# Expert feed-forward: weight rooms refilled by halves, eight groups summed in one accumulator bank, and the last choice rearranged

## Chip, cores and metric

The kernel runs on one core of a Trainium2 chip, in one launch. The metric is the device time of one execution in microseconds (us), as a median of runs. A profile of one further execution gives durations and waits; its own time stands beside it below. Engine names are those of the profile: PE (TensorE matmul), PEld (its weight loads), ACT (ScalarE), DVE (VectorE), POOL (GpSimd), SP (the engine that issues most DMAs).

## What is computed

The input x has shape [4, 128, 64, 64]: 4 batches of 4096 tokens with 128 channels, float32. Layer 0 is a convolutional attention and the first half of layer 1 a running-softmax attention with 8 heads; both are untouched. The change concerns the feed-forward at the end, where 64 experts choose tokens:

```python
logits = jnp.einsum('bsd,ed->bse', x, gate_w) + gate_b      # x: normalised tokens
probs = jax.nn.softmax(logits, axis=1)                      # over the 4096 tokens
vals, idx = jax.lax.top_k(probs.transpose(0, 2, 1), K)      # K = 8 tokens per expert
...
pooled = jnp.einsum('bked,bke->bed', gathered, topv)
h = jnp.concatenate([pooled.transpose(1, 0, 2), ones], axis=-1)
h = jax.nn.gelu(jnp.einsum('ebd,edh->ebh', h, weight1), approximate=False)
h = jnp.concatenate([h, ones], axis=-1)
out = jnp.einsum('ebh,eho->ebo', h, weight2)
...
outputs = outputs.at[jnp.arange(Bn)[:, None], flat_idx].add(weighted)
```

Each expert is 128 → 512 → 128. Per batch it sees one pooled vector, so an expert works on 4 vectors only, but its weights are 512 KB (256 KB for each of the two layers), 33.5 MB for all 64. The result is added to the tokens, and the tokens are turned back to channel-major order for the output.

## The kernel before, in words

Tokens stay in SBUF in one tile `t`, cut into NB = 32 blocks of 512 tokens (NBLK = 8 per batch, CPB = 4 chunks of 128). The gate's logits of batch b lie in `env.lg[b]` with 128 partitions (two token halves × 64 experts) and 8 × 256 columns.

The attention loop (`loop`, L2048) runs over the blocks with six blocks of lag. `make_plan` (L1989) hangs the gate's steps on slots of that loop: `gate_norm`, `gate_turn`, `gate_logits` for each block, `merge_half`, `merge_halves` (the eight best logits), `candidate_rows` (L1317, where they stand, L1321), `gathers` (L1329, POOL fetches those eight token rows by indirect DMA), `exps`, `count`, `select` and `pool` for finished batches. For the last batch all this can only end once the last block has left the attention, so `last_choice` (L1436) does it by hand: `outputs` (L1180) has made the last block; ACT takes early exponentials of the seven older blocks (`early_sums`, L1413), the gate of the last block follows (L1234, L1241, L1261, L1274, L1280, L1288), four blocks are turned back in between (`turn_early`, L1425), the candidates are weighed and spread (L1377), eight matmuls per batch with the gathered rows make the pooled vectors (L1482), the sums go through two small matmuls (L1489, L1504), and L1509 writes `f_pooled`. `put_early` (L1431) and an exponential over the whole batch (L1513) follow. `late_choice` (L1515), called by `experts`, is `count` (L1348, a check on how many tokens pass the threshold) and `select` (L1356, which zeroes all unchosen tokens in `f_lg`).

`experts` (L1570) takes the 64 experts in EG = 16 groups of QG = 4. In one group:

- `first`: four matmuls of 512 columns into a `kv` bank (L1588; the trace shows two instructions for each float32 matmul), each expert on its own 32 output partitions, then a copy by ACT (L1593);
- `turn`: four transposes (L1599), add of the bias on DVE (L1603), gelu on ACT (L1608), each over 128×512;
- `second`: 16 matmuls (32 instructions) into bank `o` (L1615), copied by DVE (L1621);
- four reloads (`load_into`, L1556): the rooms of this group's four experts are filled with the next experts not yet loaded, one DMA of 512 KB each, issued by SP;
- four matmuls with 0/1 matrices `zz` that move the group's rows to (half, expert) order and add them up over all groups in bank `t` (L1625).

On TensorE the order is `turn(g)`, two blocks turned back (`turn_back`: four transposes into bank `x` L1567, copied by ACT L1568), `first(g+1)`, `second(g)`. There is one bank `x`, so the second `turn_back` waits for the copy of the first. Twenty experts are loaded before the groups begin (some while the attention still runs), the other 44 through `load_into`. After the groups DVE scales and adds bias (L1649) into `env.eo`.

`stores` (L1654) then makes the scatter as a matmul: for each block `f_sct` = `env.eo` times the masked `f_lg` (L1660) into one of two `kv` buffers, added to the turned-back tokens by DVE (L1666), and every second block SP issues one 512 KB DMA to the output (L1669).

Order: TensorE's instructions run in the order in which the code issues them (a manual schedule, L2122 on). ACT, DVE and POOL are in code order within `loop` and `last_choice`; in `experts` and `stores` a scheduler places their instructions, and it may place one of these ahead of the last instructions of `last_choice`. `select`, `count` and the bias product L1644 are such instructions. SP's DMAs are in code order. PSUM buffers by tag: `x`, `t`, `o`, `sm` one each, `kv` two.

## Time and profile before

| | |
|---|---|
| median of three runs | 2341.73 us (2339.94 to 2343.78) |
| profiled execution, its own time | 2340.21 us |
| its span in the trace | 2338.3 us |
| mean granted TensorE clock | 0.993 |
| busy over the span: PE, DVE, ACT, POOL | 97%, 62%, 47%, 8% |
| attention loop ends on TensorE | at about 2191.7 us |
| first `first` matmul of the expert groups (f_ph, L1588) | at 2210.53 us |
| first matmul of the stores (f_sct, L1660) | at 2307.38 us |
| last output DMA issued, landed | 2331.9, about 2334.5 us |

So the part that the change touches is about the last 145 us of the span. The page's line of the TensorE clock has, for each of 40 slices of the span, the granted share of full speed in tenths (9 stands for all of it); its line of the DMA has the mean busy share of 16 DMA engines in the same slices. A row of a table of stretches names the stretch in us and its length, then for PE, PEld, DVE, ACT and POOL the busy time and the number of instructions, then the granted clock, the DMA share and the GB/s. A group row names line, engine, operation, output and inputs, shapes and count, then total busy us and mean ns of one, then the idle time just before these and what ended it. In the chain of waits each row is a start, a length and what ran: where a row follows another, the second was waiting for the first. "issue" is time in which an engine waited for nothing that the trace shows.

### The profile page before, as it was taken

The page shows a single profiled execution, that of the slowest core. Times are in us where ns is not written, and L with a number is a line of the kernel's source. Part 1 is how long each engine was busy: PE and PEld are TensorE (multiplying, and loading weights), DVE is VectorE, ACT ScalarE, POOL GpSimd, SP SyncE. Part 2 cuts the span into 40 slices and gives each one's busy share as a digit, 9 for nine tenths or more (in the row PEclk, how much of TensorE's full clock was granted, in tenths as well). Part 3 has the DMA queues.
Part 4 walks back from the last instruction along what each step waited for, and adds up shares of the span by engine and source line. Part 5 has one row for each costly group of instructions (what it writes and reads, how often), then busy time and mean ns, then how long its engine had stood idle before and what let it go on. Part 6 is the DMA issues. An engine that isn't in the chain of part 4 may idle for free.

```text
span 2338.3 us, 43371 instructions
## 1 busy us (share of the span) xinstructions
PE 2259.9 (97%) x18530; PEld 1187.3 (51%) x18530; DVE 1452.7 (62%) x2345; ACT 1095.1 (47%) x1329; POOL 183.5 (8%) x340
## 2 busy tenths in 40 slices
PE   7999999999999999999999999999999999999877
PEld 3544444444444444444444444456656656666554
DVE  7666566555665655565565555668776777865514
ACT  3343333434333443334454444455666666656531
POOL 0000000000000000000000000012122132133300
PEclk9999999999999999999999999999999999999799
DMA  2000010000010000010000000111121121143494
GB/s 80 27 12 17 9 44 12 13 8 9 17 44 9 14 11 9 9 43 9 9 5 10 5 5 5 29 42 42 38 64 50 40 73 48 40 122 96 150 356 185
DMA packets 72587, 105.82 MB, mean 45 GB/s; under 512 B 8512, under 2 KB 44352, under 8 KB 72384
## 3 DMA queue, kind: packets, MB, share of 16 engines
q1 hardware_dynamic: 70784, 99.81, 13.5%
q8 instruction: 147, 2.41, 0.4%
q0 software_dynamic: 1024, 2.10, 0.4%
q10 hardware_dynamic: 576, 1.05, 0.1%
q14 instruction: 56, 0.46, 0.1%
HBM read 79.60 MB, written 17.04 MB: 41 GB/s over the span
## 4 chain that ended last, share of the span: by engine, by line
PE 89%; DVE 5%; ACT 3%; DMA 2%; issue 1%; POOL 0%; SPq 0%; ACTq 0%; DVEq 0%; POOLq 0%
PE av L1837 37%; PE sc L1812 18%; PE f_pv L1128 9%; PE f_pk L973 8%; PE f_pt L1151 3%; PE f_po L1174 2%; PE pd L1863 1%; PE pa L1785 1%; PE pe L1759 1%; PE f_po L1185 1%; ACT f_e1a L980 1%; PE f_eo L1625 1%; DMA x<-in_x_dram 1%; PE f_ph L1588 1%; PE f_eo L1615 1%
## 5 line engine op out<-in xcount | busy, mean ns | idle before, releaser
L1837 PE MATMUL av<-pr,am 64*128 64x512 f32 x4096 | 977.6, 592 | 2.4 <-ACT pr L1817 2.4
L1817 ACT ACTIVATE pr<-sc 128x1024 f32<-128x1024 f32 x512 | 523.6, 1023 | 781.6 <-PE sc L1812 770.5
L1824 DVE TENSOR_TENSOR acc<-acc,pr 128x1024 f32<-128x1024 f32 x480 | 586.5, 1222 | 485.1 <-ACT pr L1817 480.8
L1837 PEld LDWEIGHTS av<-pr,am 64*128 64x128 f32 x4096 | 401.9, 187 | 472.8 <-issue 458.1
L1812 PE MATMUL sc<-e,e 64*128 64x512 f32 x2048 | 535.0, 591 | 3.3 <-DMA e<-side 3.3
L1812 PEld LDWEIGHTS sc<-e,e 64*128 64x128 f32 x2048 | 201.5, 187 | 234.6 <-issue 229.2
L1128 PE MATMUL f_pv<-f_held,f_ama 128*32 128x256 f32 x4096 | 237.8, 381 | 5.3 <-ACT f_e1a L980 4.6
L973 PE MATMUL f_pk<-f_held,f_ama 128*128 128x512 f32 x512 | 234.9, 603 | 0.0
L1133 ACT ACTIVATE f_amb<-f_pv 128x1024 f32<-128x1024 f32 x128 | 130.7, 1023 | 125.0 <-PE f_pv L1128 125.0
L981 DVE TENSOR_TENSOR f_e1a<-f_e1a,f_held 128x1024 f32<-128x1024 f32 x128 | 157.3, 1230 | 48.1 <-ACT f_e1a L980 47.8
L980 ACT ACTIVATE f_e1a<-f_pk 128x1024 f32<-128x1024 f32 x128 | 129.9, 1025 | 119.4 <-PE f_pk L973 55.6
L1128 PEld LDWEIGHTS f_pv<-f_held,f_ama 128*32 128x32 f32 x4096 | 129.6, 110 | 99.4 <-ACT f_e1a L980 10.9
L982 DVE TENSOR_REDUCE f_e1a<-f_e1a 128x8 f32<-128x1024 f32 x128 | 155.2, 1217 | 3.5
L973 PEld LDWEIGHTS f_pk<-f_held,f_ama 128*128 128x128 f32 x512 | 92.5, 190 | 108.6 <-issue 101.0
L1092 POOL COPY f_held<-f_e1a 32x32 f32<-32x32 f32 x128 | 30.7, 240 | 895.1 <-DVE f_e1a L1074 559.1
L1151 PE MATMUL f_pt<-f_amb,f_held 128*32 128x128 f32 x1920 | 83.6, 278 | 0.8 <-ACT f_amb L1133 0.8
L918 POOL MEMSET f_held<- 128x1024 f32 x1 | 1.0, 956 | 1036.6 <-DVE xn L1750 1036.6
L1151 PEld LDWEIGHTS f_pt<-f_amb,f_held 128*32 128x32 f32 x1920 | 60.4, 110 | 10.4 <-issue 5.2
L1190 DVE TENSOR_TENSOR t<-t,f_po 128x512 f32<-128x512 f32 x32 | 22.0, 687 | 55.6 <-PE f_po L1185 55.6
L956 ACT ACTIVATE f_xl<-t,ln_nb,ln_rs 128x128 f32<-128x128 f32 x128 | 52.8, 490 | 0.8 <-PE pa L1785 0.8
L1261 ACT ACTIVATE f_x<-t,f_gnb,f_grs 128x128 f32<-128x128 f32 x126 | 51.3, 482 | 0.4 <-DVE f_gnb L1242 0.4
L1821 DVE COPY acc<-pr 128x1024 f32<-128x1024 f32 x32 | 22.2, 694 | 39.3 <-ACT pr L1817 39.3
(269 smaller groups left out, 1835.6 us busy)
## 6 DMA issues: line engine op xcount, KB each, us to landing
f_e2a<-f_rd SPq DMA_DIRECT2D x128, 128.0 KB, 3.1
xr<-in_xtok_dram SPq DMA_DIRECT2D x32, 256.0 KB, 2.8
out_dram<-t SPq DMA_DIRECT2D x16, 512.0 KB, 3.0
f_table<-f_x SPq DMA_DIRECT2D x62, 128.0 KB, 2.2
f_held<-in_fw_dram SPq DMA_DIRECT2D x14, 512.0 KB, 6.3
f_e1a<-in_fw_dram SPq DMA_DIRECT2D x13, 512.0 KB, 6.1
x<-in_x_dram SPq DMA_DIRECT2D x12, 512.0 KB, 5.7
f_amb<-in_fw_dram SPq DMA_DIRECT2D x12, 512.0 KB, 5.8
```

The costliest lines, as they stand in the source:

```text
L956: nc.scalar.activation(xl[:, c, :], t[:, b * NCH + i, :], AF.Identity, bias=ln_nb[:, b, i : i + 1], scale=ln_rs[:, b, i : i + 1],)
L973: nc.tensor.matmul(pk[:, i, :], xt_at(n)[:, bass.ts(c, P)], env.wks[:, bass.ts(i, BLK)], start=True, stop=True,)
L980: nc.scalar.activation(flat, pk.rearrange("p i x -> p (i x)"), AF.Silu)
L981: nc.vector.tensor_mul(ks, ks, env.qb)
L982: nc.vector.tensor_reduce(s[:, (n % GB) * CPB + c, :], ks, AX.X, ALU.add)
L1128: nc.tensor.matmul(pv[a * CH : (a + 1) * CH, i, :], xt_at(m)[:, bass.ts(c * NA + i, CH)], env.wvs[:, bass.ts(a, HH * C)], start=True, stop ...
L1133: nc.scalar.activation(env.amb[:, bass.ts(c, HD)], pv.rearrange("p i x -> p (i x)"), AF.Silu)
L1151: nc.tensor.matmul(env.pt[i * CH : (i + 1) * CH, :], lhs, rhs, start=i not in env.begun, stop=False, skip_group_check=True,)
L1812: nc.tensor.matmul(sc[:, u, :], e2[halves[u], p, :], e1[halves[u], cols], start=True, stop=True,)
L1817: nc.scalar.activation(pr, sc, AF.Exp)
L1824: nc.vector.tensor_add(acc, acc, pr)
L1837: nc.tensor.matmul(av, am[h, j, :], pr[h, u, :], start=(j == 0), stop=(j == NCH - 1))
```

## The change

In `last_choice`: `early_sums` with its separate sums and `put_early` are gone. Ten blocks instead of four are turned back here (`fill`, `put_back`): six of them before the gate of the last block, into `kv`, `t` and `o`, four more between its steps; ACT or DVE copies each back. One exponential over the whole batch (ACT, L1473 of the new file) now gives the sums, and stands ahead of the pooling; the candidates are spread in two halves, the pooling matmuls four before and four after the last block's own selection, and some copies go from ACT to DVE. `outputs` adds the last block in two halves, and `candidate_rows` of the last batch is one slot earlier in the plan.

In `experts`: the rooms are refilled by halves. The first layer's half of a room (256 KB) is refilled right after `first` of its group, the second layer's half after `second`, by separate DMAs; 21 experts instead of 20 are loaded before. The second layers of eight groups accumulate in one bank: `hold` holds two tiles in which every column but the group's own four per expert is zero, so each group adds to its own rows of `env.eh`. DVE's bias add and ACT's gelu work on those columns only (128×64 in place of 128×512), POOL clears a group's columns before a tile is used again. The moving matmuls (`spread`) run twice in all, not 16 times. `turn_back` alternates between banks `t` and `x`, and 22 blocks are left to it: two per group for six groups, then one.

In `stores`: for every fifth block (six of 32) ACT copies the product out of PSUM and POOL adds it; the first two and the last two blocks are stored singly.

In the new file TensorE's order in a group is still `turn(g)`, `turn_back`, `first(g+1)`, `second(g)`. On DVE the built program has this order at the end of the last choice: copy of the selected block (L1491), first half of `count`, reciprocal of the sums (L1503), second half of `count`, L1505, `select` (L1358), L1514, the bias product, and then the product that writes `f_pooled` (L1515). Before, the two halves of `count` and `select` stood behind that product.

The diff, cut to its core:

```diff
...
+            step = CPB if m + 1 < NB else CPB // 2
...
+            for x4 in range(0, CPB, step):
+                view = t[:, bass.ds(b * NCH + k * CPB + x4, step), :]
+                nc.vector.tensor_add(view, view, env.po[:, x4 : x4 + step])
...
-        def gate_turn(m):
+        def gate_turn(m, copy=nc.scalar.copy):
...
-            nc.scalar.copy(gxt_at(m), ptr.rearrange("p c x -> p (c x)"))
+            copy(gxt_at(m), ptr.rearrange("p c x -> p (c x)"))
...
-        def early_sums():
...
-        def turn_early(n):
...
+        def fill(n, tag, half=0):
...
+            if tag == "kv":
+                if half == 0:
+                    env.two = ps.tile([P, 2, BLK], F32, tag="kv", name=f"f_etb_{n}", bufs=2)
+                dst = env.two[:, half, :]
+            else:
+                dst = ps.tile([P, BLK], F32, tag=tag, name=f"f_etb_{n}")
             for c in range(CPB):
...
+                    dst[:, bass.ts(c, P)], t[:, b * NCH + k * CPB + c, :], ident
+                )
+            fillers[n] = (env.two, half) if tag == "kv" else (dst, None)
...
+        def put_back(n, copy, count=1):
+            src, half = fillers[n]
+            at = t[:, bass.ds(n * CPB, count * CPB), :].rearrange("p i x -> p (i x)")
+            if count == 2:
+                src = src.rearrange("p n x -> p (n x)")
+            elif half is not None:
+                src = src[:, half, :]
+            copy(at, src)
...
-            early_sums()
+            act, dve = nc.scalar.copy, nc.vector.tensor_copy
+            for n, tag in enumerate(("kv", "kv", "kv", "kv", "t", "o")):
+                fill(n, tag, n % 2)
+            put_back(0, act, 2)
             gate_root(m, 1)
             gate_close(m, 1)
             gate_norm(m, split=True)
-            turn_early(0)
-            turn_early(1)
-            gate_turn(m)
...
+            put_back(2, act, 2)
+            gate_turn(m, dve)
+            fill(6, "kv")
             gate_logits(m)
-            turn_early(3)
+            put_back(4, dve)
+            fill(7, "kv", 1)
             late = st["cand"][:, bass.ts(k, 8)]
             pw = sm("f_pw1", 8)
             nc.tensor.matmul(pw, env.swap, late, start=True, stop=True)
+            fill(8, "kv")
+            fill(9, "kv", 1)
...
-            nc.scalar.activation(chd, lg, AF.Exp, bias=neg, accum_out=s31)
             st["ce"] = ce = small_tile(b, "ce", 17, bufs=1)
             nc.scalar.activation(ce, both[:, 0:17], AF.Exp, bias=neg)
-            fac = small_tile(b, "fac", 1, bufs=1)
-            nc.scalar.activation(fac, top0[:, 0:1], AF.Exp, bias=neg)
+            nc.scalar.activation(chd, lg, AF.Exp, bias=neg)
+            put_back(5, act)
+            put_back(6, act, 2)
+            st["sums"] = sums = small_tile(b, "sums", 4, bufs=1)
+            nc.scalar.activation(
+                flat_lg(b, 0, NBLK), flat_lg(b, 0, NBLK), AF.Exp, bias=neg,
+                accum_out=sums[:, 0:1],
+            )
+            put_back(8, act, 2)
+            cw = weigh_candidates(b)
+            dd = spread_candidates(cw, 0, 4)
+            spread_candidates(cw, 4, 8)
             nc.vector.scalar_tensor_tensor(
-                out=chd, in0=lg, scalar=top[:, 7:8], in1=chd, op0=ALU.is_ge, op1=ALU.mult
-            )
-            dd = spread_candidates(weigh_candidates(b))
+                out=chd, in0=chd, scalar=ce[:, 16:17], in1=chd, op0=ALU.is_ge, op1=ALU.mult
+            )
+            pp = sm("f_pp3", E)
+            for kk in range(4):
+                nc.tensor.matmul(pp, g_at(kk), dd[:, kk, :], start=(kk == 0), stop=False)
             pc = ps.tile([P, BLK], F32, tag="x", name="f_pc")
...
             ct = ex_at(1)[:, HB:].rearrange("p (j x) -> p j x", j=2)
-            nc.scalar.copy(ct, pc[:, : 2 * P].rearrange("p (j x) -> p j x", j=2))
-            pp = sm("f_pp3", E)
...
-                nc.tensor.matmul(pp, g_at(kk), dd[:, kk, :], start=(kk == 0), stop=False)
-            st["sums"] = sums = small_tile(b, "sums", 4, bufs=1)
-            nc.vector.tensor_add(sums[:, 1:2], st["e0"][:, 0:1], st["e0"][:, 1:2])
...
-                out=sums[:, 0:1], in0=sums[:, 1:2], scalar=fac, in1=s31, op0=ALU.mult, op1=ALU.add
-            )
-            pq = ps.tile([P, BLK], F32, tag="o", name="f_pq3")
+            nc.vector.tensor_copy(ct, pc[:, : 2 * P].rearrange("p (j x) -> p j x", j=2))
...
+            for h in range(2):
+                for j in range(2):
+                    nc.tensor.matmul(
+                        pp, x2[:, 2 * h + j, :], ct[:, j, h * E : (h + 1) * E],
...
-            put_early()
-            nc.scalar.activation(flat_lg(b, 0, NBLK), flat_lg(b, 0, NBLK), AF.Exp, bias=neg)
...
+        def reload1(view):
+            e = env.next1
+            if e < E:
+                env.next1 += 1
+                nc.sync.dma_start(out=view, in_=fw[e, :, :FH])
+                w1[e] = view
...
+        def reload2(view):
...
-            ptr = ps.tile([P, CPB, P], F32, tag="x", name=f"f_otr_{n}")
+            ptr = ps.tile([P, CPB, P], F32, tag="tx"[n % 2], name=f"f_otr_{n}")
...
             env.eo = env.e1b[:, 4 * BLK : 5 * BLK].rearrange("p (b c) -> p b c", b=B)
-            pe = ps.tile([P, B, C], F32, tag="t", name="f_eo")
...
+            hold = [
+                env.rest.tile([P, FC, QG, QW], F32, tag="xl", name=f"f_hs_{i}", bufs=3)
+                for i in range(2)
+            ]
+            for tile_ in hold:
+                nc.gpsimd.memset(tile_, 0.0)
...
+            def own(tile_, g):
+                at = B * (g % GH)
+                return tile_[:, :, :, at : at + B]
...
             def first(g):
                 ph = ps.tile([P, 2, BLK], F32, tag="kv", name=f"f_ph_{g}", bufs=2)
...
+                    at = (e - g % GH) * B
                     nc.tensor.matmul(
-                        ph[u * QW : (u + 1) * QW, 0, :], env.pooled[:, e * B : e * B + QW],
...
+                        ph[u * QW : (u + 1) * QW, 0, :], env.pooled[:, at : at + QW], w1[e],
+                        start=True, stop=True,
+                    )
                 nc.scalar.copy(hr, ph[:, 0, :])
-                return hr
...
+                for u in range(QG):
+                    reload1(w1[g * QG + u])
...
+            def turn(g):
...
+                if g > 1:
+                    nc.gpsimd.memset(own(hold[g % 2], g - 2), 0.0)
+                hs = own(hold[g % 2], g)
...
-                    hs, ptr,
+                    hs, own(ptr, g),
...
-                    .unsqueeze(3).to_broadcast([P, FC, QG, QW]), ALU.add,
+                    .unsqueeze(3).to_broadcast([P, FC, QG, B]), ALU.add,
...
+            def second(g):
+                if g % GH == 0:
+                    env.eh = ps.tile([P, C], F32, tag="o", name=f"f_eo_{g}")
                 for c in range(FC):
                     for u in range(QG):
                         nc.tensor.matmul(
...
+                            env.eh[u * QW : (u + 1) * QW, :], hold[g % 2][:, c, u, :],
+                            w2[g * QG + u][:, bass.ts(c, C)],
+                            start=(c == 0 and g % GH == 0), stop=(c == FC - 1 and g % GH == GH - 1),
+                            skip_group_check=True,
+                        )
...
-                    load_into(loaded[g * QG + u][2])
+                    reload2(w2[g * QG + u])
+                if g % GH == GH - 1:
+                    nc.vector.tensor_copy(env.swap, env.eh)
...
+            def spread(half, add):
+                pe = ps.tile([P, B, C], F32, tag="t", name=f"f_pe_{half}")
                 for b in range(B):
+                    at = 32 - 32 * half
                     nc.tensor.matmul(
-                        pe[:, b, :], zz[:, b, 60 - QG * g : 60 - QG * g + P], oo,
-                        start=(g == 0 and b == 0), stop=(g == EG - 1), skip_group_check=True,
-                    )
-
-            hr = first(0)
+                        pe[:, b, :], z_at[b][:, at : at + P], env.swap, start=True, stop=True,
+                    )
+                for b in range(B):
+                    nc.vector.scalar_tensor_tensor(
+                        out=env.eo[:, b, :], in0=pe[:, b, :], scalar=env.den[:, b : b + 1],
+                        in1=add[:, b, :], op0=ALU.mult, op1=ALU.add,
+                    )
...
+            first(0)
+            n = 10
...
-                for n in range(2 * g + 4, min(2 * g + 6, NB)):
+                for _ in range(2 if g < NB - 10 - EG else 1):
                     turn_back(n)
+                    n += 1
                 if g + 1 < EG:
-                    hr = first(g + 1)
+                    first(g + 1)
...
+                if g == GH:
+                    spread(0, fb2r)
+                second(g)
...
+                at = bass.ds(n * CPB, CPB)
+                view = t[:, at, :].rearrange("p (h c) x -> p h (c x)", h=2)
+                if n % 5 == 3:
+                    part = env.rest.tile([P, 2, HB], F32, tag="xl", name=f"f_scs_{n}", bufs=3)
+                    nc.scalar.copy(part, sc[:, :, :HB])
+                    nc.gpsimd.tensor_tensor(view, view, part, ALU.add)
+                else:
...
+                ends = n < 2 or n >= NB - 2
+                if ends or k % 2:
+                    lo = n if ends else n - 1
+                    at = bass.ds(lo * CPB, (n + 1 - lo) * CPB)
+                    nc.sync.dma_start(
+                        out=out[b, :, bass.ds((lo % NBLK) * BLK, (n + 1 - lo) * BLK)],
+                        in_=t[:, at, :].rearrange("p i c -> p (i c)"),
+                    )
...
             at(NB - 1, 4, pool, last)
             at(NB - 1, 4, merge_half, B - 1, NBLK - 1)
+            at(NB - 1, 4, candidate_rows, B - 1, NBLK - 1)
             at(NB - 1, "T", merge_halves, B - 1)
-            at(NB - 1, "T", candidate_rows, B - 1, NBLK - 1)
             at(NB - 1, "T", gathers, B - 1, 0, 8)
...
-            for room in (slot_of(env.ama, 0), slot_of(env.ama, 1), slot_of(env.ama, 2), env.wvs,
+            for room in (slot_of(env.ama, 0), slot_of(env.ama, 1), slot_of(env.ama, 2),
+                         slot_of(env.ama, 3), env.wvs,
```

## The prediction

> **What bounds the kernel now.** The last 145 us hold the change, so I began with the table of stretches there: which engine is full in which stage, and what the DMA does.
>
> ```profile
> 2200.00:2210.00 10.00, 7.74 (x34) 6.84 (x32) 3.32 (x16) 5.08 (x8) 2.17 (x3) 0.50 0.23 67
> 2210.00:2220.00 10.00, 8.07 (x60) 4.01 (x60) 5.74 (x8) 4.14 (x6) 0.00 (x0) 0.53 0.02 8
> 2240.00:2250.00 10.00, 8.16 (x110) 5.88 (x112) 1.67 (x3) 4.17 (x8) 0.00 (x0) 1.00 0.97 361
> 2270.00:2280.00 10.00, 7.67 (x109) 5.17 (x108) 1.83 (x4) 4.57 (x8) 0.00 (x0) 1.00 1.00 382
> 2290.00:2300.00 10.00, 7.98 (x112) 5.36 (x104) 1.97 (x4) 3.71 (x7) 0.00 (x0) 1.00 0.00 0
> 2310.00:2320.00 10.00, 8.68 (x56) 3.99 (x54) 8.63 (x14) 0.00 (x0) 0.00 (x0) 1.00 0.87 346
> ```
>
> Three things are to be seen. Around the last choice the clock is at half and the DMA idle. Between 2240 and 2280 PE works 8 of 10 us while the DMA is full (share 0.97 to 1.00) at 361 to 382 GB/s. At 2290 the loads are over, yet PE goes on at the same pace: the groups are bound by PE's own chain, with the DMA close behind. The chain of waits shows one group:
>
> ```profile
> 2275.48 0.45 PE f_otr L1567 x4
> 2275.93 0.02 issue
> 2275.95 0.59 ACT t L1568
> 2276.55 0.04 issue
> 2276.59 0.66 PE f_otr L1567 x4
> 2277.25 0.99 PE f_ph L1588 x8
> 2278.24 1.00 PE f_eo L1615 x32
> 2279.24 0.02 issue
> 2279.26 0.30 DVE f_e1b L1621
> 2279.56 0.04 issue
> 2279.61 1.16 PE f_eo L1625 x8
> 2280.76 0.44 PE f_htr L1599 x4
> ```
>
> From 2275.48 to the same point at 2281.20 is 5.72 us: 0.45 + 0.66 two blocks turned back, 0.65 the wait for the single bank `x`, 0.99 first, 1.00 second, 0.36 the copy and its gaps, 1.16 the moving matmuls, 0.44 turn. A group reloads 4 × 524,288 bytes = 2.10 MB; over 5.72 us that is 367 GB/s, just what the DMA shows.
>
> The DVE timeline shows what follows the last choice, the wait before each in brackets:
>
> ```profile
> 2207.62 0.17 DVE L1490 RECIPROCAL f_den<-f_pq 128x1 f32<-128x1 f32 x1 [3.70 <-PE f_pq L1489]
> 2210.11 0.27 DVE L1509 TENSOR_TENSOR f_pooled<-f_pp,f_e1b 128x64 f32<-128x64 f32 x1
> 2210.26 1.27 DVE L1348 TENSOR_SCALAR_CACHE_REDUCE f_e2b<-f_lg,f_ce 128x1024 f32<-128x1024 f32 x1
> 2215.01 2.34 DVE L1356 SCALAR_TENSOR_TENSOR f_lg<-f_lg,f_ce 128x2048 f32<-128x2048 f32 x1
> ```
>
> Everything waits for `f_pooled`; count and select come behind it, off the path.
>
> **What the Trainium skill says.** "TensorE: Matmul & The Clock Gate", Part 1: half rate after an idle window of about 3.4 us, full rate after about 3.4 busy us. The trace agrees with the fall: the clock goes to 0.50 at 2195.8 after 3.4 us with 1.09 us of PE work. It does not agree with the return: PE was busy from 2203.6 to 2209.8, and full clock came only at 2219.7. "DMA: Bandwidth & Descriptors", Where 436 GB/s comes from: about 358 GB/s from HBM per core, 435 as the fabric's ceiling. Here loads of 512 KB ran at 361 to 382, and for a few us around 2196 at 406 to 422, so 358 is not the limit. "PSUM — Partial Sum Buffer", The four PSUM rules, bears on accumulating across groups in one bank; no duration follows from it.
>
> **Part 1, the last choice.** Removed: `early_sums`, a table load of 1.28 and about 2.2 us of ACT, and `put_early` (1.94). Before, ACT reached the square root at 2194.89; after, a pair of blocks (1.03, as a 128×1024 copy costs elsewhere) is copied first instead, so the root is ready at 2195.1 to 2195.5. Six blocks of transposes (6 × 4 × 0.11 to 0.15 us) stand in PE's idle stretch before it. The exponentials so start at about 2201.2 against 2201.55: no real gain. The earlier `candidate_rows` (about 2 us of DVE) brings the gathers from 2193.1 to about 2190.6, but the eight rows were not the last wait. Splitting the last add gains nothing, as both halves wait for the same last matmul. Then comes what costs. ACT now does the small exponentials, 0.6 and 1.03 for three blocks, then 2.0 for the whole batch, so the sums are ready at 2205.8. DVE does the first count (1.28) to about 2207.1, the reciprocal near 2208, the second count (1.28), L1505 (0.25), select (2.34), the scale (0.23), the bias product (0.28) and then `f_pooled` (0.27). From 2208 that is 1.28 + 0.25 + 2.34 + 0.23 + 0.28 + 0.27 = 4.65, so `f_pooled` at 2212.7 to 2213. The other bound is that PE's pooling matmuls at half clock come later and end it, up to 2214.2; with a warm PE 2212.2. I take 2213.2 for the first f_ph, against 2210.53: +2.7 us. The counts are then gone from group 0, where 4.14 us of PE's work hid them anyway.
>
> **Part 2, the groups.** The PE sum per group loses the moving matmuls, copy and gaps (1.16 + 0.36) and the bank wait (0.65, of which the alternation between two banks leaves nothing: the next use of the same bank is at least 1.4 us later). From group 6 one turn-back goes too. What remains is 0.44 + 2 × 0.45 + 0.99 + 1.00 = 3.33, later 2.88 us. Add and gelu on a quarter of the old ones' width, (0.69 + 0.63) before, stay behind 0.45 + 0.99 of PE work; POOL's clearing waits for `second` of two groups back and so has a whole group; if that cover failed, some 0.5 us a group would show, still under the bound that follows.
>
> That bound is the DMA. PE at 3.3 us would need 2.10 / 3.33 = 630 GB/s, which nothing in this trace reaches. 43 experts × 524,288 = 22.5 MB are reloaded. The new unknown is the half-size load: rows of 2 KB instead of 4 KB. The nearest row is the load of x at the start, 256 KB pieces with 2-KB rows:
>
> ```profile
> 4.00:6.00 2.00, 0.00 (x0) 0.00 (x0) 1.28 (x3) 0.00 (x0) 1.48 (x9) 1.00 1.01 376
> 6.00:8.00 2.00, 0.00 (x0) 0.00 (x0) 1.84 (x5) 0.00 (x0) 0.00 (x0) 1.00 1.04 397
> ```
>
> So 376 to 397 GB/s; I take 385, with 370 and 415 as ends (the best stretch of 512 KB loads gave 406 to 422). SP needs 8 × 0.43 = 3.4 us to issue a group's eight loads, under 5.45. The start: first(0) frees its halves at once (1.05 MB, done while group 0 waits), then the stream begins after first(1). Before, first(0) to the end of first(1) took 2210.53 to 2218.81 = 8.28 us; less the bank wait 0.63 this is 7.65. Issue to first data took 1.3 us. So the stream runs from 2213.2 + 7.65 + 1.3 = 2222.2. It carries 22.5 − 1.05 = 21.5 MB, 55.8 us at 385 GB/s, to 2278.0, and 0.5 for the last landing. Behind it stand the last second, copy, spread, bias and first f_sct, 3.1 as before (2304.26 to 2307.38): 2281.6 for the first f_sct against 2307.38, that is −25.8 us. At 370 it is −23.5, at 415 −29.8.
>
> **Part 3, the stores.** Two blocks take 1.49 us: 0.73 PE, 0.70 DVE and gaps, because there are two `kv` buffers; the output runs at 346 GB/s (0.87 of the DMA). Six copies by ACT (0.585 against 0.70 on DVE) save some 0.3 us in all, and POOL's add (1.05 for the same shape elsewhere) holds up some stores by about 1 us, of which only one near the end could show. Storing the ends singly saves below 1 us. I count 0, with −2 and +2 as ends.
>
> **The sum.** 2340.21 − 25.8 = 2314.4 for the profiled execution's own time. The median was 1.5 above that execution, so 2316 us.
>
> **Rivals.**
> - *DMA at its best:* 415 GB/s, and count and select run where DVE waits anyway, so that f_pooled comes at about 2212. Then −29.8 −1.2: about 2310 us. For it: the 406 to 422 of 2196. Against: 60 us of steady stream at 369 in the same memory and rooms. Chance 0.17.
> - *Half clock:* the groups run long at 0.50. A group would cost about 5.9 us (3.33 at nearly twice, less the loads' overlap), about the DMA's 5.45; with PE pauses behind the DMA the clock might fall back again, since PE would then be busy only 3.3 of 5.45 us. Against: a stretch at 2301.6 to 2305.0 with 54% PE stayed at 1.00. It gives 2325 to 2336. Chance 0.14.
> - *Slower than before:* the half-size load has a price of its own, more outstanding DMAs for the same bytes (eight at a time are out, now 2 MB instead of 4), so the stream drops. It decides below 21.5 MB / (55.8 + 25.8 us) = 263 GB/s; at 200 GB/s the time would be 2316 + 51.7 = 2368. Against: the x loads at 376. Chance 0.05.
> - *No change:* the saved PE time comes back as the same DMA time, at 263 to 280 GB/s. Chance 0.02.
> - My forecast, 2311 to 2321: 0.62.
>
> **The numbers.** A measurement can tell about 0.2%, 4.7 us, from no change. Faster: 0.62 + 0.17 + 0.14 = 0.93; same 0.02; slower 0.05. The range for 8 in 10 reaches from the fast case (2308) to the lower part of the half-clock case (2326).
>
> **What would show it.** In the trace of the changed kernel: the first f_ph at about 2213 and behind select; a steady group period of about 5.45 us with the DMA share at 1.0 and 385 GB/s, and PE waiting for `in_fw_dram` rooms, not for ACT or DVE; no full-width copy in the groups; first f_sct near 2282; the stores' rows still at 1.49 per two blocks. I am wrong if the DMA share is below 0.9 in the groups (then something on PE's chain, the clock or the eight outstanding loads bound it), or if the first f_ph is before 2210 (then the last choice gained).

## The result, and the profile after

The changed kernel took 2319.43 us (median of 4 runs, 2316.78 to 2320.21), the kernel before 2342.76 us (4 runs): the ratio is 0.9896, 95% interval 0.9877 to 0.9915, so 23 us less. The forecast was 2316 us with a range of 2308 to 2326. The profiled execution took 2316.78 us with a span of 2315.1. Later the same kernel was run twice more, on two chips: 2331.14 us (ratio to the kernel before on the same chip 0.9951, 0.9938 to 0.9964) and 2332.14 us (0.9961, 0.9948 to 0.9973). The gain there is only 10 to 12 us, and those times lie outside the forecast's range. What happens there is told further down.

To compare executions I cut the last part at three instructions: the first of the last 32 f_po matmuls of the loop (L1185 before, L1186 after; they take 1.06 us, and "the last f_po" below means their start), the first f_ph, the first f_sct.

| stage, us | before | after | difference | forecast |
|---|---|---|---|---|
| last f_po at | 2190.64 | 2188.74 | −1.9 | 0 |
| last f_po to first f_ph (last choice) | 19.89 | 23.27 | +3.4 | +2.7 |
| first f_ph to first f_sct (groups) | 96.85 | 70.74 | −26.1 | −28.5 |
| first f_sct to end of the span (stores) | 30.92 | 32.35 | +1.4 | 0 |
| span | 2338.3 | 2315.1 | −23.2 | −25.8 |

Nearly all of the change lies behind the first row (only `candidate_rows` and one more load stand before it). Three executions of the changed kernel have that point at 2188.7, 2188.7 and 2190.6, so 1.9 us is what two executions differ by before the change is reached. In the experiments, which leave that part alone, it comes at 2188.3 to 2197.3; so whole times say less than the stages do.

The table of stretches of the changed kernel (columns as before):

```profile
2200.00:2210.00 10.00, 7.14 (x33) 6.49 (x31) 5.25 (x12) 4.47 (x6) 0.52 (x2) 0.50 0.16 52
2210.00:2220.00 10.00, 7.21 (x44) 3.79 (x48) 2.18 (x5) 3.68 (x6) 2.23 (x6) 0.50 0.34 105
2230.00:2240.00 10.00, 10.00 (x157) 7.01 (x156) 0.59 (x4) 5.51 (x12) 0.46 (x3) 1.00 1.05 388
2260.00:2270.00 10.00, 8.39 (x95) 4.73 (x96) 0.45 (x2) 2.61 (x6) 0.30 (x2) 1.00 1.04 383
2290.00:2300.00 10.00, 8.80 (x54) 3.91 (x52) 7.33 (x11) 1.28 (x3) 3.81 (x3) 1.00 0.91 358
```

From 2230 on the DMA is full, at 383 to 388 GB/s; the stores stand where the groups still ran before. PE's busy time at 2260 says little: the chain of waits shows that it waits for weights. This is the chain of the changed kernel, first a group near the start, then the last ones:

```profile
2242.26 0.62 PE f_htr L1631 x4
2242.88 0.44 PE f_otr L1583 x4
2243.32 0.99 PE f_ph L1620 x8
2244.31 0.87 PE f_eo L1649 x32
...
2255.58 5.25 DMA f_e1a<-in_fw_dram
2260.86 0.03 issue
2260.89 5.34 DMA f_ama<-in_fw_dram
2266.27 0.03 issue
2266.30 5.36 DMA f_held<-in_fw_dram
...
2277.11 1.06 PE f_eo L1649 x26
2278.17 0.58 PE f_htr L1631 x4
2278.76 0.44 PE f_otr L1583 x4
2279.19 0.28 issue
2279.47 1.30 PE f_eo L1649 x32
2280.80 0.30 DVE f_swap L1658
2281.10 0.04 issue
2281.15 1.17 PE f_pe L1664 x8
```

In the eighth group PE alone takes 2.92 us (2242.26 to 2245.19), with neither a wait for a bank nor the moving matmuls. From 2249 each link is a load that waits for the one eight before it, 5.3 us each: the groups' bound has gone from PE to the DMA. DVE's timeline at the end of the last choice:

```profile
2206.39 1.28 DVE L1350 TENSOR_SCALAR_CACHE_REDUCE f_e2b<-f_lg,f_ce 128x1024 f32<-128x1024 f32 x1 [2.96 <-PE f_pp L1497]
2207.71 1.28 DVE L1350 TENSOR_SCALAR_CACHE_REDUCE f_e2b<-f_lg,f_ce 128x1024 f32<-128x1024 f32 x1
2209.08 2.35 DVE L1358 SCALAR_TENSOR_TENSOR f_lg<-f_lg,f_ce 128x2048 f32<-128x2048 f32 x1
2211.70 0.26 DVE L1515 TENSOR_TENSOR f_pooled<-f_pp,f_e1b 128x64 f32<-128x64 f32 x1
```

Count and select now run ahead of `f_pooled`, which comes out at 2211.96, 23.2 us after the last f_po; before it was 19.7.

### The profile page after: what moved, and what is told of

It is laid out like the page before. It is cut to its first block, busy times and chain, and to the rows that moved or that the text cites. A ratio compares the mean times of both kernels' runs of the same rounds, so it can differ in the third digit from the quotient of the medians.

```text
span 2315.1 us, 43294 instructions
## 1 busy us (share of the span) xinstructions
PE 2246.9 (97%) x18418; PEld 1174.0 (51%) x18418; DVE 1439.6 (62%) x2332; ACT 1086.3 (47%) x1324; POOL 196.6 (8%) x365
## 3 DMA queue, kind: packets, MB, share of 16 engines
q10 hardware_dynamic: 576, 1.05, 0.1%
## 4 chain that ended last, share of the span: by engine, by line
PE 88%; DVE 5%; ACT 3%; DMA 3%; issue 1%; SPq 0%; POOL 0%; ACTq 0%; DVEq 0%; POOLq 0%
PE av L1887 36%; PE sc L1862 18%; PE f_pv L1128 9%; PE f_pk L973 8%; PE f_pt L1151 3%; PE f_po L1174 2%; PE pd L1913 1%; PE f_po L1186 1%; PE pa L1835 1%; PE pe L1809 1%; ACT f_e1a L980 1%; DMA x<-in_x_dram 1%; PE f_pl L1282 1%; PE otr L1925 1%; PE f_ltr L965 1%
## 5 line engine op out<-in xcount | busy, mean ns | idle before, releaser
L1128 PEld LDWEIGHTS f_pv<-f_held,f_ama 128*32 128x32 f32 x4096 | 129.5, 110 | 99.7 <-ACT f_e1a L980 10.9
L1192 DVE TENSOR_TENSOR t<-t,f_po 128x512 f32<-128x512 f32 (+1 forms) x33 | 22.1, 671 | 56.7 <-PE f_po L1186 56.7
```

What stands on the lines that cost most here:

```text
L1128: nc.tensor.matmul(pv[a * CH : (a + 1) * CH, i, :], xt_at(m)[:, bass.ts(c * NA + i, CH)], env.wvs[:, bass.ts(a, HH * C)], start=True, stop ...
```

## The experiments

Twelve kernels ran on three chips, four on each in the order given here, and the kernel before ran beside them on every chip. A kernel is compared with the kernel before on its own chip (the ratio) and, on the second and third chip, with the changed kernel there (its neighbour).

**Select behind f_pooled.** DVE's instructions of the expert stage are kept in code order, which puts count and select behind group 0's bias add.

```diff
-            experts()
+            with tc.manual_schedule(engines={mybir.EngineType.DVE}):
+                experts()
```

> The changed kernel with DVE's order in the expert stage fixed, so that both halves of the count and the select run behind the product that writes f_pooled and behind group 0's bias add. All is computed as before. Theory (these three stand on the path): from the last f_po matmul of the loop to the first f_ph it takes 19.6 us, not 23.3, since reciprocal, L1505, f_pr, L1514 and L1515 then follow f_pq at once; the groups keep their 70.7 us, so the median falls by 3 to 4 us against the changed kernel's 2319.4. Rival (PE's half clock ends the last choice, or group 0 needs DVE): f_ph comes less than 1 us sooner, or it comes sooner and the groups get longer by as much; the median stays within 1 us.

Measured: 2315.41 us (ratio 0.9899, 0.9884 to 0.9914). Last f_po to first f_ph 19.55 us, groups 73.57, stores 32.32. DVE's timeline of this kernel:

```profile
2205.93 0.17 DVE L1503 RECIPROCAL f_den<-f_pq 128x1 f32<-128x1 f32 x1 [3.21 <-PE f_pq L1502]
2207.49 0.27 DVE L1515 TENSOR_TENSOR f_pooled<-f_pp,f_e1b 128x64 f32<-128x64 f32 x1
2211.88 1.27 DVE L1350 TENSOR_SCALAR_CACHE_REDUCE f_e2b<-f_lg,f_ce 128x1024 f32<-128x1024 f32 x1
2214.51 2.35 DVE L1358 SCALAR_TENSOR_TENSOR f_lg<-f_lg,f_ce 128x2048 f32<-128x2048 f32 x1
```

The theory is right on the place: f_ph comes 3.7 us sooner, as the three instructions stood on the path. But 2.8 us of it are missing again at the end of the groups, and the two intervals of the ratio overlap, so by time alone no gain is shown. To see where they went I summed the GB/s of half-microsecond stretches from the first f_ph on. The first 5 MB landed after 21.0 us (changed kernel: 20.5), the stretch from the 5th to the 22nd MB ran at 370 GB/s (382), and the last packet of the reloads ended after 70.0 us (67.2). The first f_sct follows that packet by 3.54 us in both. So the loads alone account for the 2.8 us; group 0 took 5.47 us in both kernels and had nothing to do with it.

**Stores as before.** `stores` is that of the kernel before.

```diff
-                if n % 5 == 3:
-                    part = env.rest.tile([P, 2, HB], F32, tag="xl", name=f"f_scs_{n}", bufs=3)
-                    nc.scalar.copy(part, sc[:, :, :HB])
-                    nc.gpsimd.tensor_tensor(view, view, part, ALU.add)
...
-                ends = n < 2 or n >= NB - 2
...
+                    if k % 2:
```

> The changed kernel with the stores of the kernel before: every block added by DVE, every second block stored with its neighbour. Theory (the detour over ACT and POOL costs): from the first f_sct to the end of the span 30.9 us, as before, in place of 32.4; the median falls by about 1.4 us. Rival (the longer end comes from the DMA after the loads, whoever adds): it stays at 32 us.

Measured: 2318.54 us (0.9908, 0.9892 to 0.9923); first f_sct to the end 31.49 us, 0.9 less than the changed kernel, not 1.4. The moments within the stage tell where. With the new stores the last output DMA is issued 25.07 us after the first f_sct, with the old ones 25.29; from there to the end it takes 7.24 and 6.23. The last two kernels below show the same pair, new stores against old: 25.08 and 8.96, 25.29 and 7.94. So the detour over ACT and POOL shortens the chain by 0.2 us, and 1.0 is lost behind the last issue, where the new stores write two blocks singly. This edit takes both back at once, so the two are told apart by these moments only. An accident in this execution is worth more: the same last choice took 20.20 us from f_po to f_ph in place of 23.27, and the stretches show why:

```profile
2196.00:2200.00 4.00, 2.57 (x19) 1.70 (x18) 2.72 (x12) 1.94 (x5) 3.39 (x10) 1.00 0.78 273
2200.00:2204.00 4.00, 3.42 (x28) 3.22 (x28) 1.92 (x5) 4.00 (x6) 0.83 (x2) 1.00 0.08 16
2204.00:2206.00 2.00, 0.00 (x0) 0.00 (x0) 2.00 (x4) 0.33 (x1) 0.00 (x0) 1.00 0.69 231
2206.00:2208.00 2.00, 0.41 (x2) 0.30 (x2) 2.00 (x4) 0.00 (x0) 0.92 (x2) 0.83 0.00 0
```

The clock stayed at 1.00 until about 2207.4, so the pooling matmuls took 3.00 us in place of 5.48. In the changed kernel it was 0.50 from 2196.4 on, with the same instructions and the same pause of 1.9 us in front.

**The last choice of before.** `early_sums`, `turn_early`, `put_early` and `last_choice` are those of the kernel before; 28 blocks are left to the groups.

```diff
-            n = 10
+            n = 4
...
-                for _ in range(2 if g < NB - 10 - EG else 1):
+                for _ in range(2 if g < NB - 4 - EG else 1):
```

> The changed kernel with last_choice as it was before (early sums, four blocks turned back), and 28 blocks left to the groups: two each for twelve groups, then one. Theory (the new last choice costs 3.4 us by itself and the groups are bound by the DMA): last f_po to first f_ph 19.9 us, as before the change, groups 70.7 to 71.5 though PE has six blocks more (2.7 us), median 3 us below 2319.4. Rival (the ten blocks done early are what makes the groups short): f_ph sooner, but the groups get 2.7 us longer or more, and the median does not fall.

Measured: 2319.04 us (0.9908, 0.9893 to 0.9923). f_po to f_ph 20.55 us, groups 73.44, together 93.99 against 94.01. So the new last choice costs 2.7 us by itself, as the theory says; but the whole did not get faster, as the rival says. Of the groups' 2.7 us more, 2.5 are the loads (366 GB/s from the 5th to the 22nd MB; the last packet ended after 69.7 us against 67.2), and 0.2 lie between that packet and f_sct (3.76 us against 3.54); the first 5 MB came 1 us sooner. Whether the six additional blocks have a part in the slower loads is not separated; the run with select behind f_pooled had 370 GB/s without them.

**PE kept busy in the pause.** Sixteen more transposes into a bank in front of the gate's.

```diff
             for n, tag in enumerate(("kv", "kv", "kv", "kv", "t", "o")):
                 fill(n, tag, n % 2)
+            for c in range(4 * CPB):
+                nc.tensor.transpose(
+                    fillers[5][0][:, bass.ts(c % CPB, P)], t[:, 5 * CPB + c % CPB, :], ident
+                )
```

> The changed kernel with sixteen more transposes of one block (the same ones again, into the same bank, the result unchanged) behind the six blocks turned back at the start of the last choice, so that PE is busy from 2192.6 until the gate's transposes, where it was idle for 1.9 us. Theory (the idle stretch makes the clock fall): the clock stays at 1.00 past 2196.4, the pooling matmuls take half their 5.3 us and the first groups half of theirs; f_ph 2.5 to 3.5 us sooner, the first f_sct about 6 us sooner, median about 2313. Rival (matmuls of 64 columns count as idle): the clock falls one or two windows of 3.4 us later, during the pooling; f_ph at most 1 us sooner, and the return shifts by as much, so the groups get longer. It could even be slower by the 0.5 us for which the added transposes hold up the gate's.

Measured: 2316.99 us (0.9898, 0.9883 to 0.9913); f_po to f_ph 22.62 us, 0.65 sooner. The stretches:

```profile
2196.00:2199.00 3.00, 2.84 (x26) 2.49 (x23) 1.37 (x7) 2.53 (x6) 2.35 (x3) 1.00 1.02 385
2199.00:2202.00 3.00, 2.19 (x16) 1.25 (x14) 1.66 (x4) 2.20 (x3) 2.12 (x3) 1.00 0.94 346
2202.00:2204.00 2.00, 1.29 (x10) 1.08 (x10) 1.52 (x9) 0.74 (x3) 2.00 (x8) 1.00 0.30 84
2204.00:2206.00 2.00, 1.65 (x9) 1.65 (x10) 1.03 (x3) 2.00 (x3) 0.74 (x2) 0.65 0.00 0
```

The pause is gone, yet the clock falls at about 2204.6, 11.7 us after the last f_po where it was 7.6, while PE is busy 1.29 of 2 us. The rival holds for the clock and for f_ph: closing this one pause is not enough. The groups took 73.90 us, 3.2 more than the changed kernel's. The loads' last packet ended after 69.4 us (67.2), and 4.55 us follow in place of 3.54, as the clock fell once more at the end of the groups:

```profile
2279.70:2283.10 3.40, 1.31 (x19) 0.58 (x20) 0.00 (x0) 0.59 (x1) 0.00 (x0) 1.00 0.85 305
2283.10:2286.50 3.40, 3.40 (x39) 2.63 (x33) 0.22 (x1) 0.38 (x2) 0.00 (x0) 0.50 0.05 19
```

The profile is of the slowest of the four executions, 2323.53 us; the others took 2315.42 to 2317.85.

**The changed kernel again.**

> The changed kernel itself, beside the next ones on one chip. In its first profile the loads carried 382 GB/s between the 5th and the 22nd MB after the first f_ph, in the four experiments so far 366 to 378, and by just that their groups were longer. Theory (the groups' length is the DMA's, and its rate differs from execution to execution by some 4%): 5 MB have landed 20.5 us after the first f_ph, as in all five so far, then 17.7 MB at a rate between 365 and 385 GB/s, and the first f_sct 4 to 6 us after the last byte; groups 70.5 to 73.5 us. Rival (382 belongs to this kernel, and the edits of the experiments made the loads slower): 381 to 384 GB/s and 70.7 us again, and the experiments' slower loads are their own doing.

Measured: 2331.14 us, 12 us more than in its first runs, while the kernel before took 2343.0 there. The groups are not it: 71.08 us, with loads at 382 GB/s, as the rival said (the third run of this kernel, below, has the other figure). f_po to f_ph takes 33.13 us in place of 23.27. DVE's timeline of this execution, first instruction of the last choice:

```profile
2190.54 0.14 DVE L1317 TENSOR_SCALAR f_neg<-f_top 128x1 f32<-128x1 f32 x1
2199.24 0.75 DVE L1192 TENSOR_TENSOR t<-t,f_po 128x256 f32<-128x256 f32 x2 [8.56 <-remote]
```

PE was done with f_po at 2191.7. "remote" means that this view names nothing that ended the wait. ACT's first copy (L1431) waits too: it starts 11.6 us after the last f_po, 2.1 in the first profile, though its transposes were long done.

The packed trace tells more. Both instructions wait for PE's semaphore alone, the counter by which PE tells the others that a step is done. Times in us after the last f_po:

| | f_po, 1st | f_po, 2nd | f_po, 3rd | f_etb, 1st | DVE's add begins | ACT's copy begins |
|---|---|---|---|---|---|---|
| first profile: PE ends | 0.62 | 1.04 | 1.06 | 2.08 | | |
| first profile: count recorded | 0.66 | 1.05 | 1.13 | 2.09 | 1.15 | 2.12 |
| this run: PE ends | 0.62 | 1.04 | 1.06 | 2.35 | | |
| this run: count recorded | 2.86 | 5.74 | 8.59 | 11.54 | 8.61 | 11.56 |

So PE had done its work in time, and its counts came 2 to 9 us late; DVE and ACT went on 0.02 us after the count that they needed. What held the counts up, the trace does not say.

**Whole rooms.** Reloads of 512 KB in rows of 4 KB, all behind `second`.

```diff
-                for u in range(QG):
-                    reload1(w1[g * QG + u])
...
                 for u in range(QG):
-                    reload2(w2[g * QG + u])
+                    if env.next1 < E:
+                        load_into(rooms[g * QG + u])
```

> The changed kernel with whole rooms reloaded behind second, 512 KB in rows of 4 KB, as before the change; all else stays. Theory (halves only let the stream begin sooner; the rate is the same): the first reload begins about 6 us later, 1.0 to 1.5 MB of early loading are lost, so the first f_sct comes 3 to 5 us later relative to the first f_ph, 74 to 76 us; the median 3 to 5 us above the changed kernel's on this chip. Rival (rows of 4 KB run faster, as for the few us at 406 to 422 GB/s around 2196): 410 GB/s, 17.7 MB take 3 us less, the median within 1.5 us of the changed kernel's or below it.

Measured: 2330.45 us (0.995, 0.9936 to 0.9963), beside 2331.14 for its neighbour. Groups 73.75 us against 71.08. Stretches of this kernel:

```profile
2252.00:2262.00 10.00, 10.00 (x164) 6.78 (x156) 0.67 (x3) 4.81 (x11) 0.46 (x3) 1.00 1.02 407
2272.00:2282.00 10.00, 9.55 (x99) 4.72 (x95) 0.45 (x2) 2.42 (x7) 0.30 (x2) 1.00 1.02 408
```

Both theories had half of it. The first MB landed 6.5 us later (13.0 us after f_ph, not 6.5), as the first says. But rows of 4 KB ran at 410 GB/s where halves ran at 382, as the rival says, so the last packet ended after 66.9 us, 0.6 before its neighbour's. What is lost is behind it: 6.8 us to f_sct, not 3.55, since a whole group's first and second layer then come at the end together. So in these two executions loading by halves gained 2.7 us in the groups: less through the early start than through the short end. The medians do not show it: that of whole rooms is 0.7 us lower and the two intervals nearly coincide, as the rival said, where the theory had 3 to 5 us. And a half differs from a room in two ways, 256 KB for 512 and rows of 2 KB for 4; which of them costs the rate was not tried apart.

**The moving matmuls' work put back.**

```diff
+                nc.vector.tensor_copy(env.swap, env.eh)
+                if g % GH < GH - 1:
+                    for b in range(B):
+                        nc.tensor.matmul(
+                            env.eq[:, 1 + b % 3, :], z_at[b][:, 0:P], env.swap,
+                            start=False, stop=False, skip_group_check=True,
+                        )
```

> The changed kernel with the work of the old moving matmuls put back on PE: after each group but two the bank is copied by DVE (0.30) and four matmuls (eight instructions, 1.16 us) write a part of the bank that nothing reads. It adds 14 times about 1.5 us to PE's chain, 21 us. Theory (the DMA is the bound, PE has some 2 us of slack in each group): the groups get longer by less than 1.5 us and the median stays within 2 us of the changed kernel's. Rival (PE's chain is still the bound in the first eight groups, where PE does not wait): the first eight groups take 1.5 us more each and the first f_sct comes 8 to 12 us later.

Measured: 2339.01 us (0.9988, 0.9978 to 0.9998). Groups 80.23 us, 9.2 more than its neighbour's. My theory fell, and the rival's size is right, though every group got longer and not only the first eight. The chain of this kernel, one group:

```profile
2284.67 0.30 DVE f_swap L1658
2284.98 0.04 issue
2285.02 1.16 PE f_eo L1661 x8
2286.18 0.44 PE f_htr L1631 x4
2286.62 0.44 PE f_otr L1583 x4
2287.05 0.99 PE f_ph L1620 x8
2288.05 0.92 PE f_eo L1650 x32
```

There is no DMA in it although a group takes 4.3 us and the DMA needs 5.5 for its bytes. The next run gives the reason.

**No reload.** The two DMAs are left out, so experts 21 to 63 use the weights that lie in their rooms.

```diff
-                nc.sync.dma_start(out=view, in_=fw[e, :, :FH])
                 w1[e] = view
...
-                nc.sync.dma_start(out=view, in_=fw[e, :, FH:])
                 w2[e] = view
```

> The changed kernel without any reload in the groups: experts 21 to 63 use the weights that lie in their rooms from the experts before (so their results are those of other weights), and 22.5 MB are not moved. Theory (from group 8 on the changed kernel waits for the loads, before that for PE): the first eight groups as they were, then 2.92 us each; the first f_sct about 60 us after the first f_ph instead of 70.7, the median about 10 us lower. Rival (PE's own chain of transposes, copies and gelu is the bound): within 3 us of the changed kernel.

Measured: 2318.4 us (0.9893, 0.9879 to 0.9907), 12.7 less than its neighbour; groups 58.99 us, where the theory says 60. So the groups' chain without loads (PE and what it waits for among the engines) is 59.0 us, the loads' 71. With 14 × 1.5 = 21 us put back it is 80.0, and 80.23 was measured. That the two agree to 0.2 is partly chance: in that run the clock was at half from 2243.0 to 2246.4, where the moving matmuls, turn and two blocks turned back took 1.65 us longer than at full clock, and at the start full clock came back 6.2 us after the first f_ph, here 8.4. The two are compared as totals, not group by group: rooms for five groups stand between them, and a PE that is slower in the early groups, where no load is waited for, never makes it up. In the same way the old chain (96.85 us) would have to lose over 25 us before the loads show. Of the 26.1 us that the groups gained, 9.2 thus hang on the moving matmuls; the bank wait, the narrower add and gelu and the earlier turning back were not put back one by one.

**The changed kernel a third time.**

> The changed kernel once more, as the neighbour of the next three. On the chip of its first runs it took 10.4 us less than when it was run again on another chip, where DVE, ACT and PE stood still for 5 to 17 us at the first instructions of the last choice, for no instruction that the trace shows. Theory (a property of that chip under full DMA load): either about 23.3 us from the last f_po to the first f_ph, and 2317 to 2320, or about 33 us and 2329 to 2332; nothing in between. Rival (chance from execution to execution): a mixture of both in its five runs.

Measured: 2332.14 us (six runs, 2325.31 to 2337.93), f_po to f_ph 30.32 us, groups 72.22. Neither theory is clean: the standstill is there, but the runs spread over 12 us. The last choice is 2.8 us shorter than in the neighbour's profile above with the same standstill (ACT begins after 11.5 us), since the clock went back to 1.00 from 2208.0 to 2214.9. For the earlier question it decides: the loads of the unchanged program ran at 366 GB/s here, and 382 twice elsewhere. Stretches of this execution:

```profile
2252.00:2262.00 10.00, 10.00 (x116) 5.48 (x115) 1.72 (x7) 3.36 (x8) 0.30 (x2) 1.00 1.03 375
2262.00:2272.00 10.00, 8.20 (x94) 4.47 (x92) 0.45 (x2) 2.08 (x6) 0.30 (x2) 1.00 0.98 334
```

The DMA engines are as full as ever (0.98 to 1.03), and move less. So the 366 to 378 GB/s of the first experiments need not be their edits' doing.

**Four loads held back.** Four transposes read the rooms of `env.amb` late, so the loads wait.

```diff
             gate_logits(m)
+            for i in range(CPB):
+                nc.tensor.transpose(
+                    env.two[:, 1, bass.ts(i, P)], slot_of(env.amb, i)[:, :P], ident
+                )
```

> The changed kernel with four of the last weight loads (2 MB, the rooms of env.amb) held back until behind the gate's logits of the last block: four transposes read these rooms there into a bank that is written over after it, so the loads have to wait for them. The result is unchanged. Theory (the standstill comes from the full DMA queues): if the neighbour stands still on this chip, this one does so 5 us less or not at all, and its median is 5 to 12 us lower; if the neighbour does not, both agree within 1.5 us, since the DMA is idle for 12 us before the groups and the loads still come in time. Rival (the standstill has nothing to do with the loads): the same 33 us as the neighbour. If the loads then come too late for groups 2 and 3, it is up to 3 us slower.

Measured: 2328.93 us (0.9943, 0.993 to 0.9956), 3.2 below the neighbour's median with intervals that overlap; f_po to f_ph 30.49 us against the neighbour's 30.32. DVE's and ACT's timelines:

```profile
2197.97 0.76 DVE L1192 TENSOR_TENSOR t<-t,f_po 128x256 f32<-128x256 f32 x2 [5.68 <-remote]
...
2206.27 0.18 DVE L1243 RECIPROCAL f_grs<-f_grs 128x4 f32<-128x4 f32 x1 [5.95 <-ACT f_grs L1236]
```

```profile
2203.62 1.01 ACT L1431 COPY t<-f_etb 128x1024 f32<-128x1024 f32 x1 [17.10 <-remote]
2204.65 1.28 ACT L1236 ACT_TABLE_LOAD   x1
```

DVE waits 5.7 us in place of 8.5, but ACT starts 11.4 us after the last f_po, as ever, and all waits for ACT. From 2198.2 to 2203.2 the DMA carried 12 to 66 GB/s here. So full DMA queues are not the cause of ACT's standstill, and the theory falls.

**Halves, then whole rooms.** Experts 21 to 28 and 60 to 63 by halves, the others whole.

```diff
+        halved = lambda e: e < 29 or e >= E - QG
...
+                    if e < E and not halved(e):
+                        load_into(rooms[g * QG + u])
```

> The changed kernel with halves only where they help: experts 21 to 28 (the rooms that groups 0 and 1 free) and the last four come by halves, the 31 between by whole rooms of 512 KB behind second. Theory (rows of 2 KB ran at 382 GB/s, rows of 4 KB at 410 in the run with whole rooms): from the 5th MB on 16.3 MB at 410, so 2.8 us less; the first f_sct about 68 us after the first f_ph in place of 71, the median 2 to 3 us lower than the neighbour's. Rival (whole rooms come free later and the stream has gaps): a rate of 385 or below over the stretch and 71 us or more.

Measured: 2331.79 us (0.995, 0.9937 to 0.9963), groups 72.35 us, its neighbour's 72.22. The rate is as hoped (400 GB/s over the stretch, 408 in its middle), the last packet ends after 67.5 us and not 68.7, and 4.8 us follow in place of 3.54. The stores took 34.04 us in place of 32.31, which no run explains. By itself it gains nothing.

**All together.** Select behind f_pooled, stores as before, halves only where they help, loads held back.

> All that has helped in one kernel: the changed kernel with the select behind f_pooled, the stores of the kernel before, loads by halves only where they help, and four weight loads held back. Expected from the parts: 19.6 us from the last f_po to the first f_ph (-3.7), 68 us to the first f_sct (-2.8), 31.5 to the end (-0.9): 7 us below the changed kernel where that does not stand still, about 2312, and as much on a chip where it does, since the loads are held back. Rival (the gains overlap, as the groups' end is set by the DMA): 2315 to 2317.

Measured: 2323.32 us (0.9919, 0.9906 to 0.9931), 8.8 below the changed kernel on the same chip (0.9961, 0.9948 to 0.9973), and its interval lies below that one's: faster than both kernels there. f_po to f_ph 26.85 us (neighbour 30.32), groups 70.22 (72.22), stores 33.24 (32.34). The standstill is still in it, so holding the loads back gave nothing here; f_po to f_ph lost 3.5 us, where select's place alone had taken 3.7, and the loads' last packet ended after 65.2 us (68.7). The stages of the two profiles make up only 4.6 of the 8.8 us, as the neighbour's profile is of its fastest execution; the rest is not assigned.

## Why the prediction was right, point by point

**The sum.** 2314.4 was forecast for an execution, 2316.78 came. Between the spans the steps missed by +0.7 (last choice), +2.3 (groups), +1.4 (stores) and −1.9 (two executions differ before the change), together +2.5. That the −1.9 fell on this side is luck. It is also luck that the result was taken where the last choice does not stand still: both later medians of the same kernel lie outside the range.

**The last choice** (+2.7 forecast, +3.4 measured, for the reason given). The exponentials came 10.75 us after the last f_po, 10.91 before: "no real gain". The run with select behind f_pooled shows that count and select were the price. One term was put wrongly: I let the first count start when the sums are ready, at 2205.8, 15.2 us after the last f_po. It started 17.65 us after it, with the end of the last pooling matmul, because count writes where those matmuls read. PE at half clock and DVE's three instructions thus stand one behind the other, where I had taken the later of the two. The error stayed at 0.7 us because the reciprocal, put between the counts in the forecast too, came 1.5 us later than forecast and the work from it to the first f_ph took 0.8 less (4.4 for 5.2).

**The groups** (−28.5 forecast, −26.1 measured). PE's chain lost what I took from it: 2.92 us in the later groups against 2.88. The bound is the DMA, as said: 385 GB/s taken, 382 measured. Wrong by small sizes: the first 5 MB were there after 20.5 us, and 8.95 + 3.95 MB / 385 GB/s = 19.2 was implied; the stream ended 67.2 us after the first f_ph, and 64.8 was implied, since it also thins out behind the 22nd MB. What follows it is as counted, 3.54 us for 0.5 + 3.1. In the six profiles with these groups, all loads by halves and full clock at the end, f_sct comes 3.54 to 3.61 us after the last packet, whether that ends after 67.2 us or after 70.0: the loads set the end. It was careless to ask only whether PE is faster than the DMA per group: the run with the moving matmuls put back shows that the total over sixteen groups decides, 59 us against 71. In the forecast both gave the same answer. The steady period of 5.4 us shows only at the end, between the last four `first` (5.38, 5.38, 5.44 us); up to the eleventh group PE mostly runs at its own pace on rooms filled before.

**The stores** (0 forecast within 2, +1.4 measured). POOL's add took 1.27 us, not the 1.05 of another place. What the new stores cost is 1.0 us behind the last issue, less 0.2 gained before it, in two pairs of profiles. The other 0.6 is there with the old stores too (last issue after 25.29 us in the changed kernel, 24.48 in the kernel before), and its cause is open.

**The rivals.** Half clock: the clock was at 0.50 until 2220.2, over group 0 and part of group 1 as before, and then 1.00 to PE's last matmul at 2307.0, also where PE waited for loads; the case did not come. It is possible for a stretch: the clock fell for 3.4 us within the groups in two later executions, after 3.4 us with 1.31 us of PE work (kept busy in the pause) and with 1.74 (moving matmuls put back), and cost 1.0 and 1.65 us. Slower than before through loads of half size: the half-size load does have a price, 366 to 382 GB/s (358 with the moving matmuls put back) against 400 to 410, but 263 was needed.

**Readings.** Four readings in the forecast are slightly off, without effect on the sum: the clock before changed at 2195.56 and 2219.45 (2195.8 and 2219.7 were read), PE's share from 2301.6 to 2305.0 was 56% (54%), and the 369 GB/s are those of 2240 to 2280, while 60 us gave 357.

**What the forecast did not contain:** that the last choice can take 7 to 10 us more on other chips. No view of the kernel before showed it.

## What to carry to other kernels

When a chain is shortened, ask what the next bound is as a total over the stage and with the buffers between, not per step. An edit's gain ahead of such a bound (here 3.7 us in the last choice) is to be looked for in the stage times, since the rest differs by about as much between profiles of one kernel (1.9 us ahead of the last choice, 1.5 in the groups). And where a scheduler places some instructions, look at the order that it built: three harmless instructions stood on the critical path.

## What the runs showed of the hardware that was not expected

On two of the experiments' three chips ACT began the last choice 11.4 to 11.6 us after the last f_po in all eight profiles, and DVE 5.7 to 8.6 us; in the changed kernel's first profile and in the three experiments with this last choice on the first chip it was 2.1 and 1.15. The kernel before loses little there (2343.0 and 2342.2 us, 2341.4 on the first chip). That it is the chips, and not something else that differed, is likely but not shown. What the engines wait for is shown: PE's counts, which come late (table above). It is no late supply of instructions to DVE and ACT: ACT in all eight profiles and DVE in seven go on within 0.03 us of the count (the eighth lacks that record).

What delays the counts stays open. The standstill coincides with POOL's eight indirect DMAs, issued from 0.1 to 9.8 us after the last f_po (the change moved them ahead), and the one other wait of DVE without a releaser on these chips (L1286, 2.0 to 2.9 us) falls among four of them as well. In all eight profiles ACT starts 0.4 to 0.6 us after the last packet of the eight, which ends at 10.9 to 11.0; but the undisturbed profiles have the same DMAs at the same times. Moving `candidate_rows` back was not tried. A second rival is the recording itself: of the 128 semaphore steps by which these DMAs report, the six profiles without the standstill (the kernel before among them) have 126 to 128, the eight with it only 10 to 23, though their 128 packets of 4 bytes are all there. The record has a span and a clock for every timed execution, so whether an unrecorded one stands still is not known.

TensorE's clock fell 7.6 and 18.3 us after the last f_po in two executions with the same last choice, and with it the stage took 23.27 or 20.20 us. The same step shows with the standstill: 33.05 to 33.14 us in four profiles, where the clock was at 0.50 from 6 or 7 us on, 30.31 to 30.49 in three, where it was back at 1.00 for 6.8 us from 19.3 to 19.5 us after the last f_po. So the standstill costs 10 us and the clock 3, one beside the other. In each trace the clock's changes lie whole multiples of 3.41 us apart (in the third run 2197.80, 2208.04, 2214.86, 2225.10). The Trainium skill ("TensorE: Matmul & The Clock Gate", Part 1) says that the window over which the activity is taken is free-running, which fits.

Loads into 128 partitions, eight at a time: 256 KB in rows of 2 KB ran at 358 to 382 GB/s, 512 KB in rows of 4 KB at 400 to 410, the DMA share at about 1.0 in both. A full share is thus no measure of the rate, nor does it show what is the bound: with the moving matmuls put back it was 1.00 at 355 GB/s from 2247 to 2290, and PE set the time.
